# Transposing feed-forward rows with VectorE's 32x32 squares and DMA in place of TensorE

## The chip, the cores and the metric

The kernel runs on one core of a Trainium2 chip. A core has a matrix engine (TensorE, "PE" in the profile), three engines for elementwise work (VectorE "DVE", ScalarE "ACT", GpSimd "POOL"), and SyncE ("SP"), which computes nothing and issues DMA transfers. Each engine works through its own list of instructions in order and waits where one of them needs a result that isn't there yet. Matrix products land in PSUM, in banks of 128 partitions x 512 numbers of 32 bits; everything else lives in SBUF, 128 partitions wide. The metric is the device time of one execution in microseconds. Before the change three runs gave 747.75, 748.34 and 750.3 us, median 748.34.

## The reference

64 sequences of 64 tokens, 256 numbers each (4,096 token rows), go through four layers. Each sequence has its own conditioning vector of 64 numbers. The last two layers and the second half of the one before are what the change touches:

```
x  = L0(x)                                        # RMS norm, gated up/down product with quantization
x  = x + a_alpha * attention(ada_rmsnorm(x))      # L1, first half
x  = x + f_alpha * (silu(n @ gate.T) * (n @ hidden.T) @ out.T + out_b),  n = gamma * rmsnorm(x) + beta
x  = (x - mean) * rsqrt(var + 1e-5) * w + b ; x = (x + tanh(cond @ lin.T + lin_b)) * w + b       # L2
x  = x + relu(x @ Wd_b.T + bd) @ Wu_b.T + bu      # L3: adapter, Wd_b and Wu_b generated per sequence
```

gate and hidden are 1024 x 256, out is 256 x 1024, Wd_b is 128 x 256 and Wu_b 256 x 128.

## The kernel before

The kernel runs three phases: L0, attention, and the feed-forward phase that ends at the output. Tokens go in 8 blocks of 512 (T); the feed-forward phase starts at about 430 us of a span of 747.

A block's rows are stored in two ways. *Token-major*: a partition holds a token, four groups of 128 tokens (TT = 4) lie side by side, 256 features each. *Feature-major*: a partition holds a feature, two chunks c of 128 features, 512 tokens along the free side. A product over features needs its input feature-major; norms over a row need it token-major. So rows have to be turned between the two, 128x128 at a time, four such squares for each chunk c.

The feed-forward loop counts n = 8i + f: block i, step f of 8. Each step works on 128 of the 1024 hidden features:

- f_inner(n): f_products makes 12 products of 512 columns into two PSUM banks "gh" (four banks, so two steps' worth): gate and hidden, each as three products of a number split in a high and a low part (mm3, lines 83 to 85). ACT takes Silu of one (L796), DVE multiplies the other into it (L799, tile sg).
- f_parts(n): ACT and DVE split sg into hhi (L836) and hlo (L837).
- f_outer(n-2): 12 products of 256 columns into the banks "acc", from the hhi and hlo of two steps earlier.

Between these steps the neighbouring blocks are served:

- Block i+1 is prepared: f_load (L759, x2 from DRAM into tile fx), f_begin (ACT squares, L232, and a reciprocal root on POOL), f_scale (L247: ACT makes the normed rows xn), then norm_turn (L256 to L260): PE turns four squares of xn into a bank "mm", DVE multiplies by gamma into xg, POOL adds beta, and a split into xhf and xlf follows one step later (the list "late"). norm_turn stands at f=5 (c=0) and f=6 (c=1). The results are what f_products of block i+1 reads.
- Block i-1 is finished: at f=1 and f=2 f_scaled, f_added and f_stats (L859 to L870) take "acc" and form x3 and its row statistics; f_center (L876 on DVE makes nm, L878 is four ACT instructions) norms x3; f_adapt (L913, L914) turns x3 on PE, at f=4 (c=0) and f=5 (c=1), and DVE makes x4 out of it. At f=7 f_down (L943, 64 small products) takes x4, and f_up of block i-2 (L959) is wrapped around it: half of f_up, f_down, the other half. f_up_store (L975, L977) adds x4 and stores the output.
- Weights come by SyncE: f_rows (L271, four DMAs) at f=2, f_weights (L890 wd, L894 wu, four DMAs each) at f=6 and f=7; POOL adds a common part to them (f_common, L904) and to x2 (f_base, L780).

The last block (i=7) has no next block; its own x3 is turned by f_turn in f_last, after the loop. In f_last PE goes on to f_outer of the last two steps before f_down(6).

The order on PE, ACT, DVE and POOL in this phase is the order of the program text (manual_schedule(engines)). SyncE isn't among these engines here: the planner orders its DMAs by its own costs, so a DMA can be issued earlier or later than the text has it. The DMA of f_load, for one, is issued most of a block ahead.

Two bank tags matter: "mm" has two banks (transposes, f_down, f_up), "gh" four. SBUF tags "ex2" and "pts" (two buffers each) belong to the attention phase and are unused in this loop.

Of the kernel before, what the change touches and what calls it, by code (L numbers as in the profile page):

```python
# [8 lines left out]
F32 = mybir.dt.float32  # L9
# [3 lines left out]
ALU = mybir.AluOpType  # L13
# [4 lines left out]
P = 128  # L18
NB = 64
L = 64  # L20
D = 256
NTOK = NB * L
T = 512
NBLK = NTOK // T
BB = T // L
TT = T // P
# [6 lines left out]
V_NORM, V_AG, V_AB, V_AA, V_FG, V_FB, V_FA, V_LIN = range(8)  # L33
# [3 lines left out]
def tile_kernel(ctx: ExitStack, tc, xT, x, condT, cw, upT, downT, qkvT, woT, ghT, outT_w,  # L37
                vecs, rows, g1, g2, gb, out):
    nc = tc.nc
# [3 lines left out]
    main = ctx.enter_context(tc.tile_pool(name="main", bufs=1))  # L43
# [8 lines left out]
    pools = {}  # L52
# [7 lines left out]
    uid = [0]  # L60

    def bank(tag):
        uid[0] += 1
        tags = pools["tags"]
        if tag not in tags:
            tag = "mm"
        return pools["ps"].tile([P, 512], F32, tag=tag, bufs=tags[tag], name=f"{tag}_{uid[0]}")
# [19 lines left out]
    def b3(ap):  # L87
        return ap.rearrange("p (b l) -> p b l", l=L)
# [19 lines left out]
    E = mybir.EngineType  # L108
    engines = {E.PE, E.Activation, E.DVE, E.Pool}
    ordered = ExitStack()  # L110
# [3 lines left out]
    ident = const.tile([P, P], F32, name="ident")  # L114
# [12 lines left out]
    w2 = const.tile([P, 2], F32, name="w2")  # L127
    par = const.tile([P, 2], F32, name="par")

    def bc(v, c, i, bs=slice(0, BB)):  # L130

        n = bs.stop - bs.start
        return cv[:, v, c, i * BB + bs.start:i * BB + bs.stop].unsqueeze(2).broadcast_to([P, n, L])
# [87 lines left out]
    def rsqrt(ss, scale, eps, name, n=TT):  # L221
        ms = main.tile([P, TT], F32, tag="ms", bufs=2, name=f"ms_{name}")
        nc.gpsimd.tensor_scalar(ms[:, :n], ss, scale, eps, ALU.mult, ALU.add)
        rs = main.tile([P, TT], F32, tag="rs", bufs=2, name=f"rs_{name}")
        nc.gpsimd.tensor_tensor(rs[:, :n], ms[:, :n], nhalf[:, :n], ALU.pow)
        return rs
# [11 lines left out]
    def split(hl, c, xs, eng=None):  # L238
        nc.scalar.copy(hl[0][:, c], xs)
        (eng or nc.vector).tensor_tensor(hl[1][:, c], xs, hl[0][:, c].bitcast(F32), ALU.subtract)  # L240

    def norm_tm(xb, rs, name, scalar=False):

        xn = main.tile([P, TT, D], F32, tag="xn", bufs=1, name=f"xn{name}")
        for t in range(TT):
            if scalar:
                nc.scalar.activation(xn[:, t], xb[:, t], AF.Copy, scale=rs[:, t:t + 1])  # L247
            else:
                nc.vector.tensor_scalar(xn[:, t], xb[:, t], rs[:, t:t + 1], None, ALU.mult)
        return xn, parts(name)  # L250

    def norm_turn(xn, hl, i, c, vg, vb):

        pt = bank("mm")
        for t in range(TT):
            nc.tensor.transpose(pt[:, t * P:(t + 1) * P], xn[:, t, c * P:(c + 1) * P], ident)  # L256
        uid[0] += 1
        xg = main.tile([P, T], F32, tag="xg", bufs=2, name=f"xg{uid[0]}")
        nc.vector.tensor_tensor(b3(xg), b3(pt), bc(vg, c, i), ALU.mult)  # L259
        nc.gpsimd.tensor_tensor(b3(xg), b3(xg), bc(vb, c, i), ALU.add)  # L260
        return lambda: split(hl, c, xg, nc.gpsimd)

# [485 lines left out]
    fblk, fun = {}, {}  # L748
# [8 lines left out]
    def f_load(i):  # L757
        x2 = block(f"fx2_{i}")
        nc.sync.dma_start(out=x2, in_=tok(x2d, i))  # L759
        fblk[i] = dict(x2=x2)  # L760
# [4 lines left out]
    def f_scale(i):  # L765
        fblk[i]["n"] = norm_tm(fblk[i]["x2"], fblk[i]["rs"], f"f{i}", True)
# [15 lines left out]
    def f_products(n):  # L782
        i, f = divmod(n, 8)
        gh = pools["gh"]
        xh, xl = fblk[i]["n"][1]
        pg, pv = bank("gh"), bank("gh")
        for dst, off in ((pg, 0), (pv, FF)):
            o = slice(off + f * P, off + (f + 1) * P)
            for c in range(2):
                mm3(dst, (gh[0][:, c, o], gh[1][:, c, o]), (xh[:, c], xl[:, c]), c == 0, c == 1)  # L790
        return pg, pv

    def f_inner(n):
        pg, pv = f_products(n)
        sg = main.tile([P, T], F32, tag="st", bufs=2, name=f"sg{n}")
        nc.scalar.activation(sg, pg, AF.Silu)  # L796
        if n == LAST:
            return sg, pv
        nc.vector.tensor_tensor(sg, pv, sg, ALU.mult)  # L799
        return sg  # L800
# [60 lines left out]
    def f_added(i, k):  # L861
        B = fblk[i]
        s = slice(2 * k, 2 * k + 2)
        nc.vector.tensor_tensor(B["x3"][:, s], B["x3"][:, s], B["x2"][:, s], ALU.add)
# [7 lines left out]
    def f_center(i, tiles, rs):  # L872

        B, n, t0 = fblk[i], len(tiles), tiles[0]
        nm = pools["c"].tile([P, TT], F32, tag="nm", bufs=2, name=f"nm{i}_{t0}")
        nc.vector.scalar_tensor_tensor(nm[:, :n], B["mv"][:, t0:t0 + n, 0], -1.0, rs[:, :n], ALU.mult, ALU.mult)  # L876
        for k, t in enumerate(tiles):
            nc.scalar.activation(B["x3"][:, t], B["x3"][:, t], AF.Identity, bias=nm[:, k:k + 1], scale=rs[:, k:k + 1])  # L878
# [28 lines left out]
    def f_adapt(i, c):  # L907
        B = fblk[i]
        if c == 0:
            B["x4"] = pools["c"].tile([P, 2, T], F32, tag="x4", bufs=2, name=f"x4_{i}")  # L910
        pt = bank("mm")
        for t in range(TT):
            nc.tensor.transpose(pt[:, t * P:(t + 1) * P], B["x3"][:, t, c * P:(c + 1) * P], ident)  # L913
        nc.vector.scalar_tensor_tensor(b3(B["x4"][:, c]), b3(pt), w2[:, c:c + 1], bc(V_LIN, c, i),  # L914
                                       ALU.mult, ALU.add)

    def f_turn(i, k):
# [105 lines left out]
    turned = []  # L1023
# [40 lines left out]
    def a_norm_turn(i, c):  # L1064
        if i < NBLK:
            return norm_turn(*ablk[i]["n"], i, c, V_AG, V_AB)
        return norm_turn(*fblk[0]["n"], 0, c, V_FG, V_FB)

    late = []
    for w in range(W):  # L1070
        i, tp = divmod(w, 2)
# [36 lines left out]
        late = []  # L1108
        if tp == 0 and i + 2 <= NBLK:
            late = [a_norm_turn(i + 2, c) for c in range(2)]  # L1110
# [48 lines left out]
    bias = pools["bias"] = pools["c"].tile([P, 2, D], F32, name="bias")  # L1159
    gbt = pools["c"].tile([P, 4, D], F32, tag="yo", bufs=1, name="gbt")  # L1160
    nc.sync.dma_start(out=gbt, in_=gb)
    late = []
    for n in range(5, N):
        i, f = divmod(n, 8)
        more = i + 1 < NBLK

        for rest in late:
            rest()
        late = []
        if i > 0 and f == 2:  # L1170
            f_added(i - 1, 1)
            f_stats(i - 1, 1)
            rln = rsqrt(fblk[i - 1]["mv"][:, :, 1], 1.0, 1e-5, f"ln{i - 1}")
        sg = f_inner(n)
        if i > 0 and f in (4, 5):
            f_adapt(i - 1, f - 4)
        if more and f in (5, 6):
            late = [norm_turn(*fblk[i + 1]["n"], i + 1, f - 5, V_FG, V_FB)]
        up = i - 2 if more and f == 7 else i - 2 if not more and f == 0 else -1
        if up >= 0:  # L1180

            def between(pus):
                f_up_store(up, pus, chunks=range(1))
                if more:
                    f_down(i - 1)
            pus = f_up_products(up, between=between)
            f_up_store(up, pus, chunks=range(1, 2))
        elif more and i > 0 and f == 7:
            f_down(i - 1)
        f_parts(n, sg)  # L1190
        if n > 5:
            f_outer(n - 2, range(2 if n - 2 in KEPT else TT))
        if n == 6:
            for k in range(2):
                nc.vector.scalar_tensor_tensor(bias[:, k], gbt[:, 2 * k + 1], 0.1, gbt[:, 2 * k], ALU.mult, ALU.add)
        if i > 0:
            if f == 1:
                for k in range(2):
                    f_scaled(i - 1, k)
                f_added(i - 1, 0)  # L1200
                f_stats(i - 1, 0)
            if f == 2:
                f_center(i - 1, range(TT), rln)
        if i > 0 and more:
            if f == 0:
                f_load(i + 1)
            if f == 1:
                f_begin(i + 1)
            if f == 3:
                f_scale(i + 1)  # L1210
        if f == 2 and i > 0:
            f_rows(i)

        if f == (6 if more else 1):
            f_weights(i, "wd")
        if f == (7 if more else 1):
            f_weights(i, "wu")
        if more and f == 7:
            f_common(i, "wd", 0)
            f_base(i)  # L1220
        if i > 0 and f == 0:
            f_common(i - 1, "wd", 1)
        if i > 0 and f in (3, 4):
            f_common(i - 1, "wu", f - 3)
        if not more:
            if f == 4:
                f_base(i)
            if f in (5, 6):
                f_common(i, "wd", f - 5)
                f_common(i, "wu", f - 5)  # L1230
# [57 lines left out]
```

## Time and profile before

| what | value |
|---|---|
| median of three runs | 748.34 us |
| the profiled execution | 748.95 us, its span 746.8 us |
| granted TensorE clock, mean over the span | 1.0 of full speed |
| PE busy | 734.7 us, 98% of the span |
| DVE, ACT, POOL busy | 542.2, 405.6, 340.4 us |
| one feed-forward block in the middle, first gh product to the next block's (575.1 to 614.4 us) | 39.3 us |
| of it busy: PE, DVE, ACT, POOL | 39.0, 22.5, 16.6, 21.0 us |
| DMA in it | 0.45 of the 16 DMA engines' time, 108 GB/s |
| transposes of x3 (L913) in the loop | 56, in 14 groups of four |
| transposes of xn (L256, tile xnf), all eight blocks | 64, in 16 groups of four |

A row of a timeline gives the start, the duration, engine, line, operation, the tiles written and read, and how many instructions of a kind are joined (x4). In brackets stands the time that the engine was idle before it and whose result ended that. On PE the durations overlap, since products are pipelined; the distance between starts is what one costs. SPq rows are DMA issues: the duration is the time SyncE is held, not that of the transfer. DMA engines move the bytes afterwards, and the transfer's landing is what a reader waits for.

### The profile page before, as it was taken

The numbers are of one execution on the slowest core, as the hardware profiler recorded it, in microseconds if no ns is written. First come the engines' busy times: TensorE is split into PE (matmuls) and PEld (weight loads), VectorE is DVE, ScalarE is ACT, GpSimd is POOL, SyncE is SP. The second block draws the span as 40 slices with busy tenths as digits, with TensorE's granted clock in tenths as the row PEclk, the third lists the DMA queues.
The fourth block names the chain that finished last, engine by engine and source line by source line (L and its number), as shares of the span: only waits on it lengthen the run. The fifth ranks groups of instructions, "written<-read, shape, count | busy, mean of one in ns | idle before, by whom it ended". The sixth has DMA issues, their size and how long they took to land.

```text
span 746.8 us, 17456 instructions
## 1 busy us (share of the span) xinstructions
PE 734.7 (98%) x7036; PEld 612.1 (82%) x7036; DVE 542.2 (73%) x843; ACT 405.6 (54%) x849; POOL 340.4 (46%) x359
## 2 busy tenths in 40 slices
PE   9999999999999999999999999999999999999997
PEld 8866766777686878888888888888888888888886
DVE  4998878867687698889888876646555555565676
ACT  5553445335435588998888674535253434434242
POOL 2123133133134426765655427464646464545292
PEclk9999999999999999999999999999999999999999
DMA  8897999999995866444655237623261709080821
GB/s 258 244 265 171 270 280 231 300 278 261 229 273 108 195 153 162 113 134 122 164 150 129 79 101 183 148 52 91 63 163 32 196 4 224 1 198 2 222 62 58
DMA packets 117456, 118.87 MB, mean 159 GB/s; under 512 B 39632, under 2 KB 101200, under 8 KB 117376
## 3 DMA queue, kind: packets, MB, share of 16 engines
q1 hardware_dynamic: 109232, 91.29, 49.6%
q0 software_dynamic: 7488, 25.37, 10.9%
q10 hardware_dynamic: 656, 1.11, 0.5%
q8 instruction: 55, 0.90, 0.5%
q14 instruction: 25, 0.20, 0.1%
HBM read 71.41 MB, written 29.56 MB: 135 GB/s over the span
## 4 chain that ended last, share of the span: by engine, by line
PE 61%; DVE 17%; ACT 11%; issue 5%; DMA 3%; POOL 2%; SPq 1%; DVEq 0%; ACTq 0%; POOLq 0%
PE mm L83 9%; PE mm L85 8%; PE mm L84 8%; PE gh L85 4%; PE gh L84 4%; PE gh L83 4%; PE mm L476 3%; PE mm L298 3%; PE acc L83 2%; DMA wu<-s2d 2%; PE S L649 2%; DVE sg L799 2%; PE acc L85 2%; PE acc L84 2%; ACT x L878 2%
## 5 line engine op out<-in xcount | busy, mean ns | idle before, releaser
L83 PE MATMUL mm<-up,xhl 128*128 128x512 f32 x240 | 97.2, 405 | 0.0
L83 PE MATMUL gh<-xhf,gh 128*128 128x512 f32 x244 | 95.2, 390 | 0.0
L85 PE MATMUL gh<-xhf,gh 128*128 128x512 f32 x244 | 95.2, 390 | 0.0
L84 PE MATMUL gh<-xlf,gh 128*128 128x512 f32 x244 | 95.1, 390 | 0.0
L85 PE MATMUL mm<-up,xll 128*128 128x512 f32 x240 | 93.9, 391 | 0.0
L84 PE MATMUL mm<-up,xhl 128*128 128x512 f32 x240 | 93.6, 390 | 0.0
L799 DVE TENSOR_TENSOR sg<-gh,sg 128x512 f32<-128x512 f32 x60 | 41.3, 688 | 70.7 <-ACT sg L796 37.9
L450 ACT ACTIVATE g<-mm,rs_l 128x512 f32<-128x512 f32 x64 | 43.8, 689 | 80.6 <-PE mm L85 48.1
L837 DVE TENSOR_TENSOR hlo<-sg,hhi 128x512 fp32r<-128x512 f32 x58 | 55.2, 951 | 30.4 <-ACT hhi L836 29.5
L836 ACT CAST hhi<-sg 128x512 fp32r<-128x512 f32 x58 | 36.0, 620 | 71.9 <-DVE sg L799 71.1
L83 PE MATMUL acc<-wout,hhi 128*128 128x256 f32 x248 | 71.9, 290 | 0.0
L85 PE MATMUL acc<-wout,hlo 128*128 128x256 f32 x248 | 69.5, 280 | 0.8 <-DVE hlo L834 0.6
L451 DVE SCALAR_TENSOR_TENSOR h<-mm,rs_l,g 128x512 f32<-128x512 f32 x64 | 46.4, 744 | 32.8 <-PE mm L85 29.7
L84 PE MATMUL acc<-wout,hhi 128*128 128x256 f32 x248 | 69.3, 279 | 0.0
L260 POOL TENSOR_TENSOR xg<-xg,cv 128x512 f32<-128x512 f32 x32 | 35.3, 1114 | 71.2 <-DVE xg L259 71.2
L83 PEld LDWEIGHTS mm<-up,xhl 128*128 128x128 f32 x240 | 45.1, 188 | 15.2 <-issue 2.4
L85 PEld LDWEIGHTS gh<-xhf,gh 128*128 128x128 f32 x244 | 45.8, 188 | 9.6
L85 PEld LDWEIGHTS mm<-up,xll 128*128 128x128 f32 x240 | 45.0, 188 | 10.1
L84 PEld LDWEIGHTS mm<-up,xhl 128*128 128x128 f32 x240 | 45.2, 188 | 8.5
L83 PEld LDWEIGHTS gh<-xhf,gh 128*128 128x128 f32 x244 | 45.8, 188 | 7.3
L84 PEld LDWEIGHTS gh<-xlf,gh 128*128 128x128 f32 x244 | 45.8, 188 | 7.3
L660 DVE TENSOR_REDUCE mx<-S 128x16 f32<-128x1024 f32 x32 | 39.0, 1220 | 17.3 <-PE S L649 17.3
(220 smaller groups left out, 1929.6 us busy)
## 6 DMA issues: line engine op xcount, KB each, us to landing
gt<-in_g SPq DMA_DIRECT2D x32, 512.0 KB, 9.1
rows<-alphad SPq DMA_DIRECT2D x48, 256.0 KB, 4.8
vb<-vx SPq DMA_DIRECT2D x32, 256.0 KB, 5.1
wd<-s1d SPq DMA_DIRECT2D x32, 256.0 KB, 6.2
wu<-s2d SPq DMA_DIRECT2D x32, 256.0 KB, 6.0
xt<-in_x SPq DMA_DIRECT2D x8, 512.0 KB, 7.6
s1d<-stgs POOLq DMA_DIRECT2D x16, 256.0 KB, 8.0
s1d<-stg POOLq DMA_DIRECT2D x16, 256.0 KB, 7.9
```

The source lines that it names most:

```text
L83: nc.tensor.matmul(out, lhsT=l[0], rhs=r[0], start=first, stop=False)
L84: nc.tensor.matmul(out, lhsT=l[0], rhs=r[1], start=False, stop=False)
L85: nc.tensor.matmul(out, lhsT=l[1], rhs=r[0], start=False, stop=last)
L260: nc.gpsimd.tensor_tensor(b3(xg), b3(xg), bc(vb, c, i), ALU.add)
L298: nc.tensor.matmul(pb[s][c * 64:(c + 1) * 64], lhsT=gl[h], rhs=gt[h, c * GC:(c + 1) * GC], start=True, stop=True, tile_position=(64 * s, 6 ...
L450: nc.scalar.activation(g, pg, AF.Gelu, scale=rs[:, t:t + 1])
L451: nc.vector.scalar_tensor_tensor(h[:, ch * 512:(ch + 1) * 512], pv, rs[:, t:t + 1], g, ALU.mult, ALU.mult)
L476: nc.tensor.matmul(py[:, :D], lhsT=qt[:, f, :], rhs=wq[:, f, :], start=f == 0, stop=f == 7)
L660: nc.vector.tensor_reduce(ms, sv, AX.X, ALU.max)
L799: nc.vector.tensor_tensor(sg, pv, sg, ALU.mult)
L836: nc.scalar.copy(h_hi, sg)
L837: nc.vector.tensor_tensor(h_lo, sg, h_hi.bitcast(F32), ALU.subtract)
```

## The change

A function spread takes a token-major tile of a whole block (128 x 1024). One DVE instruction turns each 32x32 square of it where it stands: afterwards the squares are right inside, but lie on the wrong group of 32 partitions. Sixteen DMAs on SyncE's queue carry them there, one for each pair of 32 source partitions (k) and 32 target partitions (q); each reads 32 partitions, eight pieces of 32 numbers (128 bytes) from each, and writes as many: 32 KB. The result is the feature-major tile, both chunks c, in SBUF in place of PSUM. The two tiles use the tags ex2 and pts.

- x3 of every block i-1 for i from 1 to 7: the four-square transposes of f_adapt go; spread stands at f=3; DVE makes x4 from the spread tile, both chunks together at f=7 ahead of f_inner, where f_adapt had stood at f=4 and f=5.
- xn of block i+1 for i from 1 to 6: norm_spread takes the place of norm_turn at f=5 and f=6, with the same DVE, POOL and ACT instructions on the spread tile; spread stands at f=2. Block 1's rows (i = 0) still go through PE.
- f_scale moves from f=3, after f_center, to f=2, ahead of f_center.
- From the loop's start on SyncE's order is the program text's too.

In all 13 spreads take the place of 26 groups of four transposes, with 13 DVE transposes and 208 DMAs.

```diff
+    def spread(src, name):
+
+        turned = pools["b"].tile([P, 16, L], F32, tag="ex2", bufs=2, name=f"turned_{name}")
+        nc.vector.transpose(turned.rearrange("p a l -> p (a l)").rearrange("p (c t x) -> p c t x", c=2, t=TT),
+                            src.rearrange("p t (c x) -> p c t x", c=2))
+        xt = pools["b"].tile([P, 2, 512], F32, tag="pts", bufs=2, name=f"spread_{name}")
+        blocks = turned.rearrange("p (n m) (h r) -> p n m h r", m=2, h=2)
+        for k in range(4):
+            for q in range(4):
+                m, h = divmod(q, 2)
+                nc.sync.dma_start(
+                    out=xt[32 * q:32 * q + 32].rearrange("p c (t r) -> p (c t) r", t=TT)[:, :, 32 * k:32 * k + 32],
+                    in_=blocks[32 * k:32 * k + 32, :, m, h])
+        return xt
+
+    def norm_spread(xt, hl, i, c, vg, vb):
+
+        uid[0] += 1
+        xg = main.tile([P, T], F32, tag="xg", bufs=2, name=f"xg{uid[0]}")
+        nc.vector.tensor_tensor(b3(xg), b3(xt[:, c]), bc(vg, c, i), ALU.mult)
         nc.gpsimd.tensor_tensor(b3(xg), b3(xg), bc(vb, c, i), ALU.add)
         return lambda: split(hl, c, xg, nc.gpsimd)
...
-        pt = bank("mm")
-        for t in range(TT):
-            nc.tensor.transpose(pt[:, t * P:(t + 1) * P], B["x3"][:, t, c * P:(c + 1) * P], ident)
-        nc.vector.scalar_tensor_tensor(b3(B["x4"][:, c]), b3(pt), w2[:, c:c + 1], bc(V_LIN, c, i),
+        nc.vector.scalar_tensor_tensor(b3(B["x4"][:, c]), b3(B["spread"][:, c]), w2[:, c:c + 1], bc(V_LIN, c, i),
                                        ALU.mult, ALU.add)
...
+    ordered.close()
+    ordered.enter_context(tc.manual_schedule(engines=engines | {E.SP}))
...
+        if i > 0 and f == 7:
+            for c in range(2):
+                f_adapt(i - 1, c)
         sg = f_inner(n)
-        if i > 0 and f in (4, 5):
-            f_adapt(i - 1, f - 4)
         if more and f in (5, 6):
-            late = [norm_turn(*fblk[i + 1]["n"], i + 1, f - 5, V_FG, V_FB)]
+            xn, hl = fblk[i + 1]["n"]
+            if i == 0:
+                late = [norm_turn(xn, hl, i + 1, f - 5, V_FG, V_FB)]
+            else:
+                late = [norm_spread(fblk[i + 1]["turned"], hl, i + 1, f - 5, V_FG, V_FB)]
...
             if f == 2:
+                if more:
+                    f_scale(i + 1)
                 f_center(i - 1, range(TT), rln)
...
-            if f == 3:
-                f_scale(i + 1)
+            if f == 2:
+                fblk[i + 1]["turned"] = spread(fblk[i + 1]["n"][0], f"xn{i + 1}")
+        if i > 0 and f == 3:
+            fblk[i - 1]["spread"] = spread(fblk[i - 1]["x3"], f"x3_{i - 1}")
         if f == 2 and i > 0:
             f_rows(i)
```

More of the change, by code (lines that the diff above doesn't have):

```diff
@@ L259, in norm_turn @@
         nc.vector.tensor_tensor(b3(xg), b3(pt), bc(vg, c, i), ALU.mult)
+        nc.gpsimd.tensor_tensor(b3(xg), b3(xg), bc(vb, c, i), ALU.add)
+        return lambda: split(hl, c, xg, nc.gpsimd)
+    def spread(src, name):
[15 more added lines that the diff above has]
+        nc.vector.tensor_tensor(b3(xg), b3(xt[:, c]), bc(vg, c, i), ALU.mult)
         nc.gpsimd.tensor_tensor(b3(xg), b3(xg), bc(vb, c, i), ALU.add)
```

## The prediction

> **What bounds the kernel now.** I read the page's engine shares first, then TensorE's and SyncE's timelines of one feed-forward block, then DVE's and ACT's of the same stretch.
>
> ```profile
> PE 734.7 (98%) x7036; PEld 612.1 (82%) x7036; DVE 542.2 (73%) x843; ACT 405.6 (54%) x849; POOL 340.4 (46%) x359
> ```
>
> A busy PE is not proof, so I look at the spacing of steps. These rows are PE's timeline in block i=3: start, duration, operation.
>
> ```profile
> 548.15 0.39 PE L83 MATMUL gh<-xhf,gh 128*128 128x512 f32 x1
> ...
> 552.28 0.39 PE L83 MATMUL gh<-xhf,gh 128*128 128x512 f32 x1
> ...
> 556.83 0.39 PE L83 MATMUL gh<-xhf,gh 128*128 128x512 f32 x1
> ...
> 559.57 0.60 PE L913 MATMUL mm<-ident,x 128*128 128x128 f32 x4
> 560.46 0.63 PE L256 MATMUL mm<-ident,xnf 128*128 128x128 f32 x4 [0.30 <-DVE x L914]
> ...
> 562.34 0.39 PE L83 MATMUL gh<-xhf,gh 128*128 128x512 f32 x1
> ...
> 566.89 0.39 PE L83 MATMUL gh<-xhf,gh 128*128 128x512 f32 x1
> ...
> 570.70 0.99 PE L943 MATMUL mm<-x,wd 128*64 128x64 f32 x28
> ```
>
> The reader is to see steps f=3 to f=7 by their first matmul (gh), the transposes inside f=5, and f_down (L943) in f=7. A plain step takes 4.13 us (548.15 to 552.28); f=4 with one group of four transposes 4.55, f=5 with two 5.51, f=6 with one 4.55. PE issues without a gap, so in this stage PE's instructions are the time, and whatever makes PE wait adds in full.
>
> SyncE's queue decides what the change costs: a row of its timeline, then issue durations (min/median/max) of three lines, and the block's share of DMA with its GB/s (the last two columns).
>
> ```profile
> 539.21 1.94 SPq L894 DMA_DIRECT2D wu<-s2d  x3
> ```
> ```profile
> L894 SPq DMA_DIRECT2D wu<-s2d x32: 573/589/974, 448.2 to 706.6; - x32
> ```
> ```profile
> L615 SPq DMA_DIRECT2D vb<-vx x32: 591/618/1988, 249.1 to 399.9; - x32
> ```
> ```profile
> L211 SPq DMA_DIRECT2D st<-in_ghT x8: 327/340/455, 118.2 to 327.5; - x8
> ```
> ```profile
> 535.70:575.10 39.40, 39.10 (x339) 34.61 (x338) 22.60 (x36) 16.57 (x35) 21.16 (x19) 1.00 0.43 108
> ```
>
> A DMA holds SyncE 0.33 us where it spans 128 partitions (st), 0.57 us or more where it spans 64 (wu, vb); one after another, 0.65 (1.94/3). The change issues 32 more per block.
>
> **What is removed.** Four groups a block cost (4.55-4.13)+(5.51-4.13)+(4.55-4.13) = 2.22 us. Blocks i=1 to 6 lose all four: 13.3 us. Block 7 loses two single groups, 0.84. Best case 14.2.
>
> **What is added, step by step, in block i=3.** DVE's nm (L876) starts at 551.61 and takes 1.25, to 552.86. f_scale's four instructions (1.71 us on ACT), moved before f_center, fit into the 1.93 us that ACT idles before L878; they cost nothing there, and 1.7 us if that gap closed. A DVE transpose (128x1024) has no row: a 128x512 product takes 0.69 us (L799), the subtract of 128x1024 at L662 1.22, and twice that would be 2.4. I take the row of equal size, 1.22, so xn lies turned at 554.1; the ends shift each wait by -0.5 or +1.2. The second runs after hlo(3), from 557.6 to 558.8. DVE has room (22.6 of 39.4 us busy); without it, 2.4 us a block.
>
> Then SyncE, now in program order: 16 DMAs for xn, 4 for f_rows, 16 for x3. Let p be the time of one of the 16. Of the rows 4 x 0.65 = 2.6. The last x3 DMA starts at 554.1+31p+2.6 and lands 2.3 us after its start (the last out_y took 1.8 to 2.1 with little in flight; behind 256 KB transfers rows take 4 to 6, which would add up to 3.7 a block; by then the four f_rows transfers are ten issues old, so I take a value near the low end). f_adapt's two instructions follow (0.74 long, started 0.61 apart as L859's are: 1.35). x4 is ready at 560.35+31p. PE's f_down today starts after half of f_up, at 570.70; without transposes it would start at 570.70-2.22 = 568.48. PE then waits 31p-8.13 us, every block, with f_up's second half, f_outer(5) and the whole next block behind it.
>
> p has no row of its own (32 partitions, eight pieces of 128 bytes each). Lower end: st's 0.33 plus a 0.05 gap, 0.38. Upper end by the data: with traffic at 108 GB/s and a DMA share of 0.43 in this block, 39.4 us carry 4.26 MB; in pieces of about 1 KB that is 4,160, each 39.4 x 16 x 0.43/4,160 = 65 ns. If a piece of 128 bytes cost as much, 16 per DMA engine would give 1.04 us. I take 0.65: issue durations follow the partition span, vb is also SBUF to SBUF, and 128 bytes are unlikely to cost what 1 KB does. So the wait is 31 x 0.65-8.13 = 12.0 us. Block: +12.0-2.2 = +9.8; six blocks: +58.8.
>
> Before that, xg of f=5, which needs all 16 pieces for either half, waits on DVE until the xn spread lands: 554.1+15 x 0.65+2.3 = 566.2, against about 562. Behind it queue hlo(5), sg(6), hlo(6) and f_adapt; PE needs hlo(5) only after f_down, so these 4 us hide under the 12.
>
> Block 7: x3 turned after hlo (716.39+1.51) and a transpose, 719.1; SyncE is idle; x4 ready at 719.1+15p+2.3+1.35 = 722.75+15p = 732.5. f_adapt now stands ahead of the last sg (L831, 727.35 before), for whose h_lo PE waits: +5.2 (the 0.84 is inside it).
>
> Other moves: f_load was issued a block ahead (544.83, used in the next block); in program order it comes at f=0, behind two out_y and four wu, and lands some 8.5 us later, about when f_begin's squares are due. I price it 0; a miss costs ACT 1 to 2 us, which two steps of slack cover. f_weights (wd) goes behind the x3 spread, and POOL's f_common, f_base and next rsqrt behind its landing: covered by the same wait; without it 2 to 3 us on POOL, which PE doesn't see for a block. The other DMAs keep their count.
>
> **TensorE's clock.** No idle of PE over 1.1 us exists in this trace, so its aftermath must be bounded. At the start PE is cold:
>
> ```profile
> 7.10 2.05 PE L432 MATMUL mm<-up,xhl 128*128 128x512 f32 x4
> 8.95 0.79 PE L432 MATMUL mm<-up,xll 128*128 128x512 f32 x2
> 9.57 1.09 PE L432 MATMUL mm<-up,xhl 128*128 128x512 f32 x4
> 10.50 0.63 PE L432 MATMUL mm<-up,xll 128*128 128x512 f32 x2
> ```
>
> Four matmuls take 1.85 us (7.10 to 8.95), later 0.93 (9.57 to 10.50). PE's first matmul stands at 1.0, so the slow state lasted at most 8.3 us and cost at most half of it, 4.1. Per wait 0 to 4.1; I take the middle, 2.0: six times 12.
>
> Sum on the profiled execution, 748.95 (span 746.8 and 2.15 around it): 748.95+58.8+5.2+12 = 825. The median of the runs shown is 0.6 lower: 824.
>
> [...]
>
> **Rivals.** *The transfers are hidden (faster).* If p is below (8.13+2.22)/31 = 0.33, the wait is smaller than the saving; with no wait the time is 748.95-14.2 = 734.8. For it: SyncE issues nothing for 27 us of each block (471.3 to 498.7), and st issues in 0.33. Against: no shorter span than 128 partitions issues so fast. *A short wait.* p at 0.38 to 0.50: the wait is 3.7 to 7.4, total 758 to 783 (blocks 6 x 1.4 to 6 x 5.2, block 7 1.1 to 2.9), up to 12 more with the clock. *The pieces bound the spread, not the issue.* p 0.8 to 1.04: wait 16.7 to 24.1; 855 to 904. For it: pieces of 128 bytes where the kernel has moved 512 or more in this stage. *DVE becomes the bound:* 2.4 us more on 22.6 in a block of 37.2 leaves 12 spare, so I give it no chance of its own; if it did, the block could not pass 37.2 by more than those 2.4, 749 in all.
>
> **Numbers.** Likeliest (p 0.5 to 0.8, clock 0 to 4.1 per wait): 0.61, own range 783 to 868. Short wait 0.18. Pieces 0.12. Hidden 0.07, and 0.02 for a tie near p=0.33. Changes within 0.3% can't be told from none in this kernel. The range 758 to 875 reaches to the low ends of p and into the pieces' case; it leaves out the hidden one, the tie and most of the pieces'. Faster 0.07, same 0.02, slower 0.91.
>
> **What the profile after would show.** No L913 in PE; a PE gap of some 12 us before L943 in six blocks, ended by DVE x (f_adapt), which was ended by a DMA; SyncE nearly continuous for 23 us from f=3 on; DVE idle before xg; matmuls of 0.45 spacing after the gap if the clock falls. I am wrong if SyncE issues 32 partitions in under 0.4 us, or if x4 is not what PE waits for.

## The result, and the profile after

The changed kernel takes 828.99 us (median of four runs, 828.42 to 831.13) against 748.05 for the kernel before beside it: 1.108 times as long, 95% interval 1.105 to 1.111. The profiled execution is 829.22 us, its span 827.4, 80.6 more than before.

The page's engine shares and its row of granted clock:

```profile
PE 738.3 (89%) x6932; PEld 615.3 (74%) x6932; DVE 547.4 (66%) x856; ACT 405.8 (49%) x849; POOL 343.1 (41%) x359
...
PEclk9999999999999999999999996979979699796998
```

PE runs 104 instructions fewer and yet is busy 3.6 us longer, in a span of which it now leaves 11% idle; from the 25th of the 40 slices on its clock falls every two or three slices. The view of waits names who waited for whom: total us, how often, the longest.

```profile
PE mm L963 <- issue: 72.0, 6, 13.6
POOL xg L283 <- DVE xg L282: 66.5, 12, 11.3
...
DVE x L934 <- DMA spread_x<-turned_x: 50.4, 7, 8.7
...
DVE xg L282 <- DMA spread_xn<-turned_xn: 30.1, 6, 5.8
...
PE acc L83 <- ACT hhi L855: 4.6, 1, 4.6
```

L963 is f_down, six times 12.0 us. The view calls the releaser "issue"; the timelines of block i=2 show whom it really waited for. SyncE, DVE and PE in turn, with the start, the duration and the operation:

```profile
528.58 10.44 SPq L273 DMA_DIRECT2D spread_xn<-turned_xn  x16
539.06 2.61 SPq L294 DMA_DIRECT2D rows<-alphad  x4
541.77 10.43 SPq L273 DMA_DIRECT2D spread_x<-turned_x  x16
```
```profile
540.64 0.69 DVE L282 TENSOR_TENSOR xg<-spread_xn,cv 128x512 f32<-128x512 f32 x1 [4.82 <-DMA spread_xn<-turned_xn]
...
553.68 1.41 DVE L934 SCALAR_TENSOR_TENSOR x<-spread_x,w,cv 128x512 f32<-128x512 f32 x2 [7.59 <-DMA spread_x<-turned_x]
```
```profile
542.03 1.15 PE L979 MATMUL mm<-dn,wu 128*64 128x64 f32 x32
554.53 4.08 PE L963 MATMUL mm<-x,wd 128*64 128x64 f32 x64 [11.35 <-issue]
558.40 1.92 PE L979 MATMUL mm<-dn,wu 128*64 128x64 f32 x32
```

SyncE is held from 528.58 to 552.20 almost without a break. The last DMA of x3's spread starts at 551.59; DVE begins x4 at 553.68, and f_down follows 0.85 us later, after PE had idled for 11.35. The same block cut at the wait's two ends and behind f_down: the stretch, PE's busy time, the other engines', then the granted clock, the share of DMA and GB/s.

```profile
510.30:543.00 32.70, 32.70 (x214) 28.68 (x212) 17.75 (x29) 12.66 (x29) 13.11 (x12) 1.00 0.25 57
543.00:554.50 11.50, 0.18 (x7) 0.04 (x2) 2.87 (x5) 2.72 (x5) 4.06 (x3) 0.66 0.53 108
554.50:558.40 3.90, 3.73 (x64) 3.57 (x66) 1.85 (x3) 0.00 (x0) 1.57 (x2) 0.50 0.89 272
558.40:561.80 3.40, 3.40 (x50) 3.28 (x48) 0.95 (x2) 1.20 (x2) 3.40 (x4) 0.73 0.03 9
```

The clock falls inside the wait and is still at half when f_down runs: its 64 products take 3.77 us from first to last start, against 1.82 at full clock. Blocks 1 to 6 took 234.1 us together and now 308.1, 74.0 more; the seventh and the tail take 6.4 more.

### The profile page after: what moved, and what is told of

It is laid out like the page before. It is cut to its first block, busy times and chain, and to the rows that moved or that the text cites. A ratio compares the mean times of both kernels' runs of the same rounds, so it can differ in the third digit from the quotient of the medians.

```text
span 827.4 us, 17523 instructions
## 1 busy us (share of the span) xinstructions
PE 738.3 (89%) x6932; PEld 615.3 (74%) x6932; DVE 547.4 (66%) x856; ACT 405.8 (49%) x849; POOL 343.1 (41%) x359
## 4 chain that ended last, share of the span: by engine, by line
PE 28%; SPq 14%; DVE 13%; ACT 7%; issue 5%; DMA 4%; POOL 1%; DVEq 0%; ACTq 0%; POOLq 0%
SPq L273 14%; PE mm L83 3%; PE mm L85 3%; PE mm L963 3%; PE mm L84 2%; PE gh L85 2%; PE gh L84 2%; PE gh L83 2%; PE S L672 2%; PE mm L713 2%; DMA spread_x<-turned_x 2%; PE acc L83 2%; ACT ex L690 1%; PE acc L85 1%; DVE sg L822 1%
## 5 line engine op out<-in xcount | busy, mean ns | idle before, releaser
L83 PE MATMUL mm<-up,xhl 128*128 128x512 f32 x240 | 97.2, 405 | 0.0
L83 PE MATMUL gh<-xhf,gh 128*128 128x512 f32 x244 | 95.2, 390 | 0.0
L963 PE MATMUL mm<-x,wd 128*64 128x64 f32 x448 | 25.8, 304 | 72.8 <-issue 72.0
L963 PEld LDWEIGHTS mm<-x,wd 128*64 128x64 f32 x448 | 23.6, 212 | 75.0 <-issue 73.0
L822 DVE TENSOR_TENSOR sg<-gh,sg 128x512 f32<-128x512 f32 x60 | 40.9, 682 | 53.2 <-PE gh L85 28.6
L83 PE MATMUL acc<-wout,hhi 128*128 128x256 f32 x248 | 71.4, 288 | 4.6 <-ACT hhi L855 4.6
L860 DVE TENSOR_TENSOR hlo<-sg,hhi 128x512 fp32r<-128x512 f32 x58 | 47.1, 812 | 35.6 <-ACT hhi L859 35.3
L927 POOL TENSOR_TENSOR wd<-wd,bias 128x512 f32<-128x512 f32 x32 | 44.3, 1405 | 45.5 <-DMA wd<-s1d 45.5
L83 PEld LDWEIGHTS mm<-up,xhl 128*128 128x128 f32 x240 | 45.1, 188 | 15.2 <-issue 2.4
L85 PEld LDWEIGHTS gh<-xhf,gh 128*128 128x128 f32 x244 | 45.8, 188 | 9.6
L83 PEld LDWEIGHTS acc<-wout,hhi 128*128 128x128 f32 x248 | 47.3, 191 | 7.4 <-ACT hhi L855 4.8
```

The lines of the kernel that those rows point to most:

```text
L83: nc.tensor.matmul(out, lhsT=l[0], rhs=r[0], start=first, stop=False)
L85: nc.tensor.matmul(out, lhsT=l[1], rhs=r[0], start=False, stop=last)
L860: nc.vector.tensor_tensor(h_lo, sg, h_hi.bitcast(F32), ALU.subtract)
L927: nc.gpsimd.tensor_tensor(w[:, 2 * h:2 * h + 2], w[:, 2 * h:2 * h + 2], row.unsqueeze(1).broadcast_to([P, 2, D]), ALU.add)
L963: nc.tensor.matmul(pd[s * 64:(s + 1) * 64, (b - b0) * L:(b - b0 + 1) * L], lhsT=B["wd"][b // 4][:, b % 4, c, s * 64:(s + 1) * 64], rhs=B[" ...
```

## The experiments

The theory: SyncE needs 0.65 us for each of the 16 DMAs of a spread, x3's spread stands last in its queue, and f_down waits for it. The rivals: the bytes or the 128-byte pieces take the time; DVE does; the new order does. The ratios below are to the kernel before, run beside each on the same chip, with 95% intervals.

### The number of DMAs: four_wide, eight_64, long_pieces

```diff
-        for k in range(4):
-            for q in range(4):
-                m, h = divmod(q, 2)
-                nc.sync.dma_start(
-                    out=xt[32 * q:32 * q + 32].rearrange("p c (t r) -> p (c t) r", t=TT)[:, :, 32 * k:32 * k + 32],
-                    in_=blocks[32 * k:32 * k + 32, :, m, h])
+        for k in range(4):
+            m, h = divmod(k, 2)
+            nc.sync.dma_start(out=xt.rearrange("p c (t r) -> p (c t) r", t=TT)[:, :, 32 * k:32 * k + 32],
+                              in_=blocks[:, :, m, h])
```

> The changed kernel with each spread made by 4 DMAs over all 128 partitions in place of 16 over 32: the same bytes in the same pieces of 128 bytes, the same DVE turning, but every square stays on its partitions, so the values downstream are those of other rows. Queue theory: 4 issues of 0.4 to 0.55 us, both spreads land before they are needed, no PE wait, full clock, all of the transposes' 14.2 us gained: 734 to 736. Piece theory (128-byte pieces limit the transfer): as many pieces take as long as before, above 800. DVE theory (turning or SBUF reading slows DVE until PE waits): 745 to 760.

Measured: 744.99 us, 0.995 (0.993 to 0.998), 84 us less than the changed kernel with the same bytes in the same pieces. The theory that the pieces bound the spread falls, and so does DVE's as the cause of the 81 us, for DVE has the same work here. But it isn't the 735 that the queue theory gave; it stands at the lower end of the 745 to 760 of the DVE theory. Three things stand between: TensorE still waits 0.4 to 1.1 us in four blocks, 0.75 and 3.39 in the tail, and the clock falls once, behind the tail's wait. Part of this is DVE's after all: the waits of 1.0 and 1.1 us (blocks 3 and 5) are for f_adapt's second instruction, which took 1.84 and 1.76 us there instead of 0.75, and the 3.39 in the tail stands behind two more such instructions. The last section shows what they ran beside. L272 is the spread; shortest, median and longest issue in ns:

```profile
L272 SPq DMA_DIRECT2D spread_x<-turned_x x28: 617/678/3193, 483.7 to 713.9; - x28
L272 SPq DMA_DIRECT2D spread_xn<-turned_xn x24: 593/674/702, 477.9 to 669.0; - x24
```

A DMA over 128 partitions does not issue faster here than one over 32 (0.609 in the changed kernel), and in each of the six blocks one of x3's four is held for 2.4 to 3.2 us. That hold became a question of its own, below.

eight_64 carries each spread by 8 DMAs of 64 partitions:

```diff
+            for s in range(2):
+                m, h = divmod(k, 2)
+                hs = slice(64 * s, 64 * s + 64)
+                nc.sync.dma_start(out=xt[hs].rearrange("p c (t r) -> p (c t) r", t=TT)[:, :, 32 * k:32 * k + 32],
+                                  in_=blocks[64 - 64 * s:128 - 64 * s, :, m, h])
```

> The changed kernel with each spread carried by 8 DMAs of 64 partitions instead of 16 of 32: the same bytes in the same 128-byte pieces, but half of the values come to wrong partitions, so x4 and the normalized input are wrong. Theory (SyncE's time per DMA, 0.65 us whatever the partitions, sets the wait): the normalized rows' spread takes 5.2 us of SyncE and x3's 5.2, so f_down starts 10.4 us earlier than in the changed kernel, which leaves 0.2 to 1.6 us of the 11.6 us wait in each block and a tail like that of the four-DMA kernel (some 4 us): 748, from 743 to 757. Rival (the bytes or pieces are what takes long): near 829. Second rival (a DMA over more partitions takes SyncE longer in proportion, 1.3 us for 64): near 829 as well, with half as many issues of twice the length in the trace.

Measured: 768.85, 1.027 (1.024 to 1.030). Halving the DMAs takes 60 of the 81 us away, so the time goes with their number; an issue takes 0.634 us, not 1.3. It missed the 748 because x3's eight take 5.7 to 6.5 us from first to last start and not 4.7 (some of them are held, up to 2.25 us), so f_down waits 2.5 to 3.0 us in five blocks and 5.2 in one, and because the clock falls behind four of these six waits, which I had not expected of so short ones.

long_pieces keeps 16 DMAs of 32 partitions, each with one piece of 1 KB per partition:

```diff
+        flat = turned.rearrange("p a l -> p (a l)")
...
+                nc.sync.dma_start(out=xt[32 * q:32 * q + 32].rearrange("p c n -> p (c n)")[:, 256 * k:256 * k + 256],
+                                  in_=flat[32 * k:32 * k + 32, 256 * q:256 * q + 256])
```

> The changed kernel with the same 16 DMAs of 32 partitions and the same bytes, but one piece of 1 KB per partition and DMA instead of eight of 128 bytes; the values land in wrong places. Theory (SyncE's time per DMA alone): unchanged, 829 within 3, with 16 issues of 0.61 us and the same waits of 11 to 13 us. Rival (the number of pieces makes the issue or the landing long): an issue of 0.3 us or less, waits under 4 us, time below 780.

Measured: 818.53, 1.093 (1.090 to 1.096). An eighth of the pieces, and an issue is 0.588 us instead of 0.609. Of the 10 us gained, 31 x 0.02 us a block are the shorter issues (3.7 in all). Much of the rest has another source: x3's first chunk now arrives with the first eight DMAs, so f_adapt's first instruction (0.75 us) and four products of f_down run inside the wait, which splits in two (5.5 and 4.4 us in block 2). The pieces' rival is out here too.

### One spread at a time: xn_only, x3_only

xn_only returns x3 to TensorE at f=4 and f=5:

```diff
-        if i > 0 and f == 7:
-            for c in range(2):
-                f_adapt(i - 1, c)
         sg = f_inner(n)
+        if i > 0 and f in (4, 5):
+            f_adapt(i - 1, f - 4)
...
-        if i > 0 and f == 3:
-            fblk[i - 1]["spread"] = spread(fblk[i - 1]["x3"], f"x3_{i - 1}")
```

x3_only returns the normalized rows at f=5 and f=6:

```diff
-            if i == 0:
+            if True:
                 late = [norm_turn(xn, hl, i + 1, f - 5, V_FG, V_FB)]
...
-            if f == 2:
-                fblk[i + 1]["turned"] = spread(fblk[i + 1]["n"][0], f"xn{i + 1}")
```

> The changed kernel with x3 turned by PE at f=4 and f=5 as before; only xn goes by DVE and DMA. Queue theory: f_adapt needs no spread, so the wait before f_down is gone and the clock stays full. xn still lands 12 us after its first issue and xg waits for it on DVE to the same point of the block (some 18 us after f=3's first product); Silu of f=7 stands on ACT behind the cast of the second xg, so yo's first half comes late and PE waits some 3.9 us before f_up's second half (two mm banks) in blocks 2 to 6: 748 - 6 x 1.4 + 5 x 3.9 = 759, 752 to 763. Rival, each spread alone is hidden and only the sum of both is too long: 740.

> The changed kernel with xn turned by PE as before; only x3 goes by DVE and DMA. Queue theory: 16 issues of 0.65 us start when x3 is turned, last landing 12 us later; x4 is ready some 2.9 us after PE reaches f_down in blocks 1 to 6 (no clock fall expected at that length), against 1.4 us saved: +1.5 x 6; block 7 keeps its +5 to +8 at the end. 762 to 765. Rival, a fixed cost of any x3 spread (data pieces, DVE's turning) that does not shrink with the queue: a wait near 12 us in each block again, above 800.

Measured: 774.38, 1.034 (1.031 to 1.037), and 775.85, 1.036 (1.031 to 1.041). Each part alone costs a third of the whole, 26 and 27 of 81 us: the parts don't add up, because both stand in one queue and the second pays for the first. Both came out 11 us above the upper end of what was expected. These waits were as expected (2.1 to 3.5 us before f_down with x3 alone; 3.4 to 4.6 before f_up's second half with xn alone), but not the clock behind them; xn_only also waits 1.54 and 0.86 us at the start of block 2, which was not forecast. Two rows of x3_only, from blocks 2 and 5:

```profile
536.64 3.45 PE L963 MATMUL mm<-x,wd 128*64 128x64 f32 x64 [2.14 <-DVE x L934]
...
665.07 2.40 PE L963 MATMUL mm<-x,wd 128*64 128x64 f32 x64 [2.23 <-DVE x L934]
```

After a wait of 2.14 us the 64 products took 3.45 us, after one of 2.23 us 2.40. The granted clock fell to half for 3.4 us in the first case and not at all in the second.

In xn_only x3's spread is gone and with it the wait of f_down, and a wait comes forward that the changed kernel had hidden:

```profile
DVE xg L282 <- DMA spread_xn<-turned_xn: 32.0, 6, 6.0
...
PE mm L982 <- DVE yo L998: 19.7, 5, 4.6
```

DVE works in order: xg waits for the rows, the eviction yo stands behind it, and f_up's second half needs the PSUM bank that yo empties. In the changed kernel the same xg waits as long (30.1 us in all) and costs nothing, since f_down waits longer.

### The clock by itself: warm_fill

```diff
+        pb = bank("gh")
+        for _ in range(count):
+            nc.tensor.matmul(pb, lhsT=pools["gh"][0][:, 0, 0:P], rhs=xh[:, 0], start=True, stop=True)
...
+                    f_fill(i, 45)
                     f_down(i - 1)
```

> The changed kernel with 45 additional products of 512 columns, whose result nothing reads, between the first half of f_up and f_down at f = 7 of six blocks, so that TensorE works through most of the wait for x4; some 10 us of work in a wait of 11.3 to 13.6. Theory (after each wait TensorE runs at half its clock for about 4.5 us, which costs 2.3 us a block): the clock stays at 1.0 and the time falls by 6 x 2.3 = 14 to 815. Rival (the clock's fall costs nothing, since the queue sets the pace after the wait too): 829. If the additional work is longer than the wait: over 829.

Measured: 821.86, 1.097 (1.094 to 1.101): 7.1 us less, half of what the theory gave. f_down's products, in ns, first in the changed kernel, then here:

```profile
L963 PE MATMUL mm<-x,wd x448: 222/314/369, 504.5 to 815.5; 128*64 128x64 f32 x150
```
```profile
L969 PE MATMUL mm<-x,wd x448: 222/222/271, 504.9 to 806.9; 128*64 128x64 f32 x150
```

The clock stays at 1.0 in all six blocks. From f_down's start to the next block's first gate product the six blocks take 28.6 us together instead of 39.8, which is 1.9 a wait: that is the price of the clock. The 7.1 comes out smaller since f_down, counted from each block's start, begins later, 3.3 us over the six blocks (in four of them one issue of x3's spread was held for 1.2 to 2.0 us), and the stretches ahead of block 1 and behind block 6 are 0.7 us longer.

At full clock the 28.6 us are still 3.2 more than the 25.4 of the kernel before. Block 2 of warm_fill shows why:

```profile
554.01 0.34 PE L969 MATMUL mm<-x,wd 128*64 128x64 f32 x4 [0.86 <-issue]
554.63 1.97 PE L969 MATMUL mm<-x,wd 128*64 128x64 f32 x60 [0.28 <-DVE x L934]
```

f_down starts behind the first of f_adapt's two instructions, runs four products and waits for the second. In the kernel before x4 was long complete when f_down began; here this costs some 0.5 us in each of the six blocks, in the changed kernel too.

### What holds SyncE: four_late

```diff
-        if f == 2 and i > 0:
+        if f == 3 and i > 0:
             f_rows(i)
...
-        if i > 0 and f == 7:
+        if more and i > 0 and f == 7:
             for c in range(2):
                 f_adapt(i - 1, c)
         sg = f_inner(n)
+        if not more and f == 7:
+            for c in range(2):
+                f_adapt(i - 1, c)
```

> The kernel with four DMAs of 128 partitions a spread (the values land on wrong partitions), and two more edits: the four DMAs of the rows are issued after x3's spread instead of before it, and in the last block f_adapt stands behind the gate's product instead of ahead of it. Theory (the hold of 2.5 us on x3's third DMA comes from the rows' transfers ahead of it in the queue, and the tail's wait of 3.4 us from f_adapt's place): no issue of x3's over 1 us, no wait of TensorE over 0.5 us ahead of f_down, none over 1 us in the tail: 738, from 736 to 741. Rival (the hold is the spreads' own, by their 128-byte pieces): the hold stays, and the time falls by the tail's 4 us alone, to 741 or more.

Measured: 747.36, 0.998 (0.996 to 0.999). SyncE in block 3, first with four_wide's order, then with this one; below them all issues of x3's spread in this kernel:

```profile
554.20 2.69 SPq L292 DMA_DIRECT2D rows<-alphad  x4
556.98 4.61 SPq L272 DMA_DIRECT2D spread_x<-turned_x  x4
```
```profile
555.10 2.79 SPq L272 DMA_DIRECT2D spread_x<-turned_x  x4
557.93 2.68 SPq L292 DMA_DIRECT2D rows<-alphad  x4
```
```profile
L272 SPq DMA_DIRECT2D spread_x<-turned_x x28: 594/680/702, 481.9 to 709.5; - x28
```

The hold is gone: it came from the rows' transfers (256 KB each) ahead in the queue, not from the spread's pieces. Four of the six blocks now take 37.12 us against 39.3 before, the 2.2 us that the prediction gives for the transposes, with next to no wait left. The tail's wait ahead of L83 is gone too. But the total missed the 738, for in the last block the rows now come later too:

```profile
POOL fx L801 <- DMA rows<-alphad: 12.4, 1, 12.4
...
DVE nm L897 <- POOL rs_ln L225: 8.3, 1, 8.3
```

POOL waits 12.4 us for them, the reciprocal root that f_last's norm needs is queued behind that wait, and PE idles 10.27 us, with the clock at half for 10.2 us. The same move in blocks 1 to 6 alone wasn't tried.

### The order alone: order_only, scale_early

order_only is the kernel before with SyncE in program order and f_scale ahead of f_center, without any spread; scale_early has the second edit alone:

```diff
             if f == 2:
+                if more:
+                    f_scale(i + 1)
                 f_center(i - 1, range(TT), rln)
...
-            if f == 3:
-                f_scale(i + 1)
```

> The kernel before with only the two moves of order: SyncE in the order of the program text from the loop's start, and f_scale ahead of f_center at f=2. PE turns all rows as before. Queue theory (the 36 DMAs in series are the cost): nothing is late, 748 us, within 2. Rival, the order itself costs (f_load late, f_weights behind waits): above 755, with ACT waiting for fx or POOL for wd before PE does.

> The kernel before with one edit: f_scale is written ahead of f_center at f = 2 instead of at f = 3, and SyncE's order stays the planner's. Theory (the 0.5 us a block that the kernel with the new order gained at f = 5 comes from f_scale, which no longer stands on ScalarE ahead of the work that the transposes' bank waits for): 745.5 within 1, the step at f = 5 of 5.0 us instead of 5.5. Rival (the gain comes from SyncE's written order): 748.5 within 1.

Measured: 745.50, 0.996 (0.994 to 0.998), and 745.48, 0.995 (0.994 to 0.997). Neither order costs anything, and moving f_scale gains 0.4%, in the step f=5: 4.99 us instead of 5.5. ACT and then PE, before:

```profile
479.95 1.70 ACT L247 ACTIVATE xnf<-fx,rs_f 128x256 f32<-128x256 f32 x4
481.56 0.58 ACT L796 ACTIVATE sg<-gh 128x512 f32<-128x512 f32 x1
```
```profile
482.76 0.60 PE L913 MATMUL mm<-ident,x 128*128 128x128 f32 x4
483.66 0.63 PE L256 MATMUL mm<-ident,xnf 128*128 128x128 f32 x4 [0.30 <-DVE x L914]
```

and PE with f_scale moved:

```profile
481.96 0.60 PE L913 MATMUL mm<-ident,x 128*128 128x128 f32 x4
482.39 0.60 PE L256 MATMUL mm<-ident,xnf 128*128 128x128 f32 x4
```

f_scale's 1.70 us stood ahead of a Silu; DVE's product of that Silu came late, f_adapt's x4 behind it on DVE came late, and the second group of transposes waited for the bank that it empties. Moved, ACT does it in a gap that it had anyway, and the two groups follow each other 0.43 us apart. SyncE's order has no part in the gain. With this edit, and with all transposes on TensorE, these two kernels are the fastest here with every value in its place.

### Fewer DMAs with the values in place: dram, xn_dram, gather_first

A spread by way of device memory needs five DMAs: one store of 128 partitions and four gathers of 32.

```diff
+        td = dram.tile([P, 2 * T], F32, name=f"td_{name}")
+        nc.sync.dma_start(out=td, in_=turned.rearrange("p a l -> p (a l)"))
...
+        src = td.rearrange("(k a) (n q r) -> q a n k r", k=4, q=4, r=32)
+        for q in qs:
+            nc.sync.dma_start(out=xt[32 * q:32 * q + 32].rearrange("p c (t k r) -> p (c t) k r", t=TT, k=4),
+                              in_=src[q])
```

> The changed kernel with VectorE's turning kept, but each spread carried as one DMA over 128 partitions into device memory and four DMAs of 32 partitions back, placed so that no DMA waits for the one just issued: 5 issues for each instead of 16, same values. Theory (SyncE's time per DMA): x3's last piece starts at about the same time as with four DMAs straight across, so f_down waits under 1.5 us in each block and the tail pays some 4 us: 745, from 737 to 757. Rival (a round trip through device memory takes longer than the SyncE time it saves, 2 us more for each landing than seen so far): waits of 2 to 4 us in each block with the clock's fall behind them, 760 to 775.

Measured: 783.02, 1.046 (1.043 to 1.049), worse than either side expected. f_down waits 4.0 to 5.6 us, with 6.8 us of half clock around each wait. And it isn't x3's spread that is late: f_adapt never waits for a DMA in this trace. xg does, 29.0 us in six waits, and f_adapt stands behind it on DVE. x3's store was held 2.3 to 2.7 us on SyncE in six blocks and the second half of the rows' gathers behind it. The longer landing of the rival is there as well: the last of the rows' gathers lands 3.6 to 4.8 us after its start, where the pieces of the changed kernel took 1.9.

So the next two versions return x3 to TensorE and carry only the normalized rows, first with the gathers behind the rows' four DMAs (xn_dram), then ahead of them (gather_first).

> A version meant to beat both: x3 turned by TensorE as before, the normalized rows turned by VectorE and carried by one DMA into device memory and four back, the four rows DMAs between the store and the gathers, so that SyncE issues 5 DMAs for it instead of 16. Theory (SyncE's queue was all that made the changed kernel slow, and five DMAs for the rows that are needed last fit into it): no wait of TensorE over 1 us in any block, the clock stays up, and against the kernel before with the new order (745.5) two groups of four transposes go in each of six blocks, 0.9 us a block: 740, from 737 to 744. Rival (SyncE's weights loads come late all the same, as with the normalized rows alone by 16 DMAs, and f_up waits 1 us or more in each block): 750 to 765.

> The version with the normalized rows alone by way of device memory, with one edit: the four gathers are issued ahead of the four DMAs of the rows, so that SyncE waits some 3 us for the store's landing with nothing queued ahead of the gathers. In the run without this edit, the multiplication that reads the gathered rows came 5.6 us late on VectorE, and the eviction behind it on the same engine held the PSUM bank that f_up's second half waits for by 4.3 us, some 1.3 less. Theory (the gathers are late because the rows' transfers are queued ahead of them): they land some 4 us earlier, VectorE waits about 1.4 us, TensorE 0.2 at most, the clock stays up, and two groups of transposes, 0.9 us, are gone from each of six blocks against the kernel with f_scale moved (745.5): 740.5, from 738 to 746. Rival (the gathers of 128-byte pieces are slow by themselves, 1.3 us or more each): TensorE still waits 2 us or more a block, 755 to 765.

Measured: 770.00, 1.026 (1.022 to 1.030), and 746.72, 0.996 (0.995 to 0.998). SyncE in block 2 of each, then the waits of each (the profiled execution of gather_first, 749.69 us, is its longest of eight):

```profile
515.54 2.62 SPq L297 DMA_DIRECT2D rows<-alphad  x4
518.25 5.15 SPq L277 DMA_DIRECT2D spread_xn<-td_xn  x4
```
```profile
516.06 2.91 SPq L277 DMA_DIRECT2D spread_xn<-td_xn  x4
519.02 3.15 SPq L297 DMA_DIRECT2D rows<-alphad  x4
```
```profile
DVE xg L285 <- DMA spread_xn<-td_xn: 28.0, 6, 5.6
...
PE mm L985 <- DVE yo L1001: 17.0, 5, 4.3
```
```profile
DVE xg L285 <- DMA spread_xn<-td_xn: 12.7, 6, 3.1
...
PE mm L985 <- DVE yo L1001: 5.2, 4, 1.9
```

Two lines in another order are worth 23 us. Ahead of the rows the gathers take 2.91 us of SyncE instead of 5.15. gather_first is faster than the kernel before, but not than scale_early, whose interval overlaps its own and whose move it contains, so that carrying the rows by DMA gained nothing that these runs show; its 740.5 was missed because the gathers still land 3.3 to 5.3 us after the last one's start and TensorE still waits 0.5 to 1.9 us in four blocks.

## Why the prediction was right, step by step

The forecast was 824 and the result 829, and the likeliest case was the one that came. Its steps:

- *The transposes' 2.22 us a block.* Right: steps f=0 to f=6 of the changed kernel are 4.13 us each, in all six blocks, and four_late's undisturbed blocks are 2.2 shorter than before.
- *p = 0.65 per DMA.* Right: 0.653 from start to start. The argument for it was half wrong. I had read the time off the partition span (0.33 over 128, 0.57 or more over 64) and expected four_wide to issue faster; its DMAs over 128 partitions take 0.674. In these runs 0.33 belongs to 128 partitions in one piece each (dram's store of the rows, 0.332), and eight pieces each cost 0.67. That the value held is luck as far as it rests on the span.
- *The four rows DMAs 2.6, landing 2.3 after the last start, the DVE transpose 1.22, f_adapt 1.35.* Measured 2.61, 1.9, 1.23 and 1.41. The wait 31p-8.13 = 12.0 came out at 11.29 to 13.57, on average 12.0. So close a hit is partly luck: the landing came 0.4 us earlier, f_down began behind f_adapt's first instruction (0.85 us after its start) and not behind both (1.35), and SyncE needed 0.3 to 1.5 us more for the 36 DMAs; these nearly cancel. f_down's second wait of 0.5 us, for f_adapt's second instruction, was not foreseen.
- *xg's 4 us, hidden under the wait.* Right (4.8 in block 2), and xn_only shows the price without the cover: its wait less 1.25 us falls on TensorE.
- *f_load's later place, f_scale's move, POOL's and f_weights' later work at nothing.* No wait of theirs reaches TensorE in the changed kernel. f_scale's move gains where there are transposes to gain for.
- *Block 7, +5.2.* Measured 6.4: waits of 0.76 and 4.58 us in place of 0.60, less 0.84 for its transposes, and some 2.5 for 4.9 us of products at half clock behind the second wait. That last term was missing: I priced the clock six times and there are seven waits. The waits without it come to 3.9, less than the 5.2, so the two errors partly cancel.
- *The clock, 2.0 a wait, taken as the middle of 0 to 4.1.* Measured 1.9 by warm_fill. The middle of a range is no mechanism, and that it fits is luck. What I didn't see is where it begins: the trace had no wait over 1.1 us, and I spoke only of waits of 12. In eight_64, x3_only and xn_only waits of 2 to 5 us paid it too (2.14 us was enough in one block of x3_only, 1.73 in one of gather_first), and this is a large part of why those three expectations failed (in eight_64 the waits were longer than expected as well).
- *The sum.* For blocks 1 to 6, waits 72.0, clock 11.1 and f_down's second waits 3.2 (28.6 less 25.4, in warm_fill) less the 13.3 that the transposes' absence saves there are 73.0 of the 74.0 measured; 0.2 us a block is not assigned. The forecast for these blocks was 58.8+12 = 70.8; the 3.2 us that it lacks are as much as those second waits.
- *The rivals.* Hidden transfers needed p under 0.33; four_wide shows the queue's part removed otherwise, and even that gives 745 and not 734.8. The pieces as the bound are refuted by four_wide and long_pieces. DVE as the bound was to end at 749 at most, and the result is 829; what DVE does cost, f_adapt slowed to up to 1.84 us, shows in four_wide, where the queue's wait is gone.

## What to carry to other kernels

An operation that left the critical engine for DMA paid here per DMA issued, not per byte (829, 769 and 745 us with 16, 8 and 4 DMAs a spread and the same bytes): multiply their number by what SyncE is held for each (0.59 to 0.67 us here), add what stands ahead of them in the queue, and hold the landing against the time when the first consumer would otherwise start. Look at what is queued behind every waiting instruction on an in-order engine, for hidden waits come forward as soon as the longest is removed (19.7 us in xn_only), and price each new idle gap of TensorE twice, with the clock behind it (1.9 us a wait in warm_fill). And try moving a small piece of work into another engine's idle gap first: one such move gained at least as much here as any version of the idea that keeps the values in place.

## What the runs showed of the hardware

- *The clock after short waits.* Counted over all runs, blocks 1 to 6 only: of the waits under 1.7 us no single one was followed by half clock (one pair in xn_only, 1.54 and 0.86 in close succession, was); in gather_first it fell after 1.73 us and not after 1.85; from 2.1 to 3.0 it fell after seven of ten, from 3.0 to 4.0 after nine of ten, above that each time (after 11.29 to 13.57 in the changed kernel). The half-clock stretches last 3.4 us (x3_only), 6.8 (dram, and the tail of the changed kernel), 10.2 (four_late) or 13.65 (the changed kernel, each of the six blocks). Why it fell after 2.14 us and not after 2.23 in x3_only, no run here shows.
- *Issue times on SyncE.* Medians of the spreads' DMAs: 32 partitions, one piece each 0.588 (long_pieces), eight 0.609 (the changed kernel). 64 partitions, eight pieces 0.634 (eight_64). 128 partitions, eight pieces 0.674 to 0.678 (four_wide), one piece 0.332 (dram's store of the rows). With the rows' four DMAs of 256 KB ahead of x3's spread in the queue, a single issue was held up to 3.193 us (four_wide); with them behind it 0.702 at most (four_late).
- *DVE beside POOL.* f_adapt now reads the spread tile and a second operand from SBUF; beside an idle POOL it takes 0.75 us, like its form reading PSUM before (0.74). Beside a busy one it took up to 1.84. All f_adapt instructions of four_wide, in ns:

```profile
L932 DVE SCALAR_TENSOR_TENSOR x<-spread_x,w,cv x14: 737/914/1840, 491.0 to 722.3; 128x512 f32<-128x512 f32 x14
```

In these runs who began first decides. Block 4 of four_late shows both cases, POOL's addition of L281, the two f_adapt instructions and POOL's subtraction of L240:

```profile
600.89 1.50 POOL L281 TENSOR_TENSOR xg<-xg,cv 128x512 f32<-128x512 f32 x1 [0.63 <-DVE xg L280]
```
```profile
601.41 2.19 DVE L932 SCALAR_TENSOR_TENSOR x<-spread_x,w,cv 128x512 f32<-128x512 f32 x2
```
```profile
603.12 1.63 POOL L240 TENSOR_TENSOR xlf<-xg,xhf 128x512 fp32r<-128x512 f32 x1 [0.73 <-ACT xhf L239]
```

L281 was under way when the first f_adapt came; that one took 1.53 us and ended 0.55 us after L281. The second took 0.74, and L240, which began during it, took 1.63 instead of 1.3. So it is in all runs: each of the 24 f_adapt instructions that took over 1 us met a POOL instruction that had begun before the DVE instruction ahead was done (xg's addition as in L281, the weights' additions, or in blocks 3 and 5 of four_wide L240), and ended 0.55 us after it. In the kernel before, two f_adapt instructions of block 7, reading PSUM, ran beside such additions and took 0.73.

In the tail of four_wide two f_adapt instructions, 1.76 and 1.75 long, stand ahead of the last step's work and make the wait of 3.39 us there.
